# Last scan of a recurrent convolution: columns of the second pair written to the output 32 at a time, in place of store, read back and shuffle

## The chip, the cores and the metric

One core of one Trainium2 chip. The metric is the device time of one execution in microseconds (us), the median of several executions. Times inside the profile are counted from the first instruction of one profiled execution.

## What is computed

The program is four residual layers on x of shape (4, 48, 256, 256), float32: an attention layer, a gated layer, and two layers of directional scans. Only the last of the scan layers matters here. After a group normalisation it runs four scans, each a recurrence with a convolution of width 5 over the 48 channels, and the result is added to x:

```python
def step(w, b):
    def f(carry, inp):
        nxt = inp + _conv1d(carry, w, b)
        return (nxt, nxt)
    return f
...
r0 = ws[0]
_, r_rest = jax.lax.scan(step(right_w, right_b), r0, ws[1:])
R = jnp.concatenate([r0[None], r_rest], 0)
l0 = R[Ww - 1]
_, l_rest = jax.lax.scan(step(left_w, left_b), l0, R[Ww - 2::-1])
L = jnp.concatenate([l0[None], l_rest], 0)[::-1]
return jnp.moveaxis(L, 0, 3)
...
x = x + _L3_conv_ref(_gn(x), ...)
```

The four scans go down the rows, up the rows, right over the columns and left over the columns. Step t needs step t - 1, so one scan of 256 steps is a strict chain. The left scan of the last layer yields the output, column 255 first and column 0 last; the output lies in memory row by row.

## The kernel before

The four images are two pairs of two. A pair has its own `chain` (a Python generator, one `yield` per scan step). A step (`step`, L1037) is done for each of the two images: three matmuls of 96x96 on 96x128 (L1045), a VectorE add of the step's input out of PSUM into one of four carry buffers (L1053 for column scans, L1049 for row scans), and a third operation that keeps the result. The 96 partitions are 48 channels times the parity of the position along the vector; for a column, partition half r holds the rows 2h + r.

The chains are interleaved by hand at the end of `scans` (from L1373). Chain 0 leads by LEAD = 992 steps, then both run alternately, step by step, until chain 0 is done. Chain 1 then runs its last 992 steps alone: nearly all of its last layer, whose left scan comes last.

Instructions go into each engine's queue in an order that a planner works out from the order of the program, from what they depend on and from when buffers come free; it may send a load out earlier than the program has it. All large transfers of this stage are issued by SyncE (SP), on one DMA queue.

The left scan (L1268 to L1306) takes the 256 columns in 16 blocks of 16, block 15 first. Per block it needs two tiles of 96 partitions times 16 KB (1536 KB each): `lines`, the right scan's results, from R (L1273), and `stage`, the layer's input x of the same columns, from x (L1274). Both are asked for a block ahead. In every step GpSimd (POOL) adds the new carry into `stage` in place (L1282), in pieces of 96x128; the elements of one column stand 32 bytes apart in `stage`. When a block is done, `stage` is stored (L1291) to a tensor `y` in memory, in a column-blocked layout with runs of 8 columns (32 bytes) of one row.

`to_rows` (L1337) brings `y` into the row layout of the output. It loads pieces of `y` (`oi`, L1348), shuffles them with copies on POOL, VectorE (DVE) and ScalarE (ACT) into `oo` (L1364 to L1368), and stores `oo` to `out` (L1370). Its arguments choose the pair, the blocks of columns and the buffers. The loop over chain 1 (L1383 to L1397) calls its pieces between steps:

- pair 0, all columns, a piece every 32 steps;
- at step lead - W // 2 = 864, when the left scan of pair 1 is halfway, what is left of pair 0, and from then on the right half of pair 1 (finished by then), a piece every 10 steps;
- after the last step, what is left, and then the left half of pair 1 with the buffers of both pairs.

Buffers: each pair has a ring of five slots of 16 KB a partition (`take`, L1012), and a slot is taken again when its last user is done. While chain 1 runs alone, its own five hold `lines` and `stage`, and those of pair 0 hold `oi` and `oo`. `SLOT` is 4096 elements, `CB` 16 columns, `NK` 16 blocks, `KC` 8.

Of the kernel before, what the change touches and what calls it, by code (L numbers as in the profile page):

```python
# [16 lines left out]
B, C, H, W = 4, 48, 256, 256  # L17
G = 16
NP = 2
# [5 lines left out]
KC = 8  # L25
NK = W // (2 * KC)
# [88 lines left out]
def rows(pair):  # L115
    return slice(pair * P, (pair + 1) * P)
# [848 lines left out]
def scans(ctx, tc, xs, out, wts, biases, dram, k, coefs, lead, spare):  # L965
# [13 lines left out]
    nc = tc.nc  # L979
# [19 lines left out]
    CB = 2 * KC  # L999
    SLOT = 2 * NK * NH * KC  # L1000
# [11 lines left out]
    def take(pair, name):  # L1012
        return buffers[pair].tile([P, SLOT], F32, tag="slot", name=name)

    def chain(pair):
# [8 lines left out]
        def slot(name):  # L1024
            return take(pair, f"{name}{pair}")

        def inner():
            return carry[at[0]][:, :, 1 : HP - 1]
# [27 lines left out]
        def rows_view(t):  # L1056
            return t.rearrange("p (b k h w) -> p b k h w", b=2, k=NK, w=KC)

        def cols_view(t):
            return t.rearrange("p (b q h w) -> p b q h w", b=2, q=2, w=KC)  # L1060

        def lines_view(t):

            return t.rearrange("p (w b h) -> p w b h", w=CB, b=2)

        def row(ts, r):
            return rows_view(ts[r % 2])[:, :, :, r // 2, :]

        def load_rows(layer, n, ts, k0, k1):

            for r in range(2):
                v = rows_view(ts[r])
                for q in range(2):
                    for b in range(2):
                        nc.sync.dma_start(
                            v[q * C : (q + 1) * C, b, k0:k1].rearrange("c k h w -> c k (h w)"),
                            xs[layer][pair][
                                r * C : (r + 1) * C, b, 2 * k0 + q : 2 * k1 - 1 + q : 2, n * NH : (n + 1) * NH, :
                            ].rearrange("c k h w -> c k (h w)"),
                        )  # L1080

        def layer_of(layer, first):
# [6 lines left out]
            block_of = lambda x, n: x[:, :, 2 * n : 2 * n + 2].rearrange("p b q h w -> p b (q h w)")  # L1089
            by_batch = lambda t: t.rearrange("p (b n) -> p b n", b=2)  # L1090
# [3 lines left out]
            for b in range(2):  # L1094
                t = home.tile([P, 2], F32, tag=f"biased{pair}{b}", name="biased", bufs=2)
# [19 lines left out]
            for n in range(NT):  # L1115
                ahead_ = None
                for r in range(RT):
# [3 lines left out]
                    if ahead_ and r >= RT // 2 and r % 4 == 0:  # L1121
                        i = (r - RT // 2) // 4
# [3 lines left out]
                    def keep(new, b):  # L1126
                        nc.scalar.activation(inp[:, b], blocks(new[:, b]), AF.Identity, bias=bias[:, 0:1])  # L1127
# [15 lines left out]
            for n in reversed(range(NT)):  # L1143
                ahead_ = None
                for r in reversed(range(RT)):
# [4 lines left out]
                    if n == 0 and r == RT // 4:  # L1150

                        column = slot("col")
                        v = cols_view(column)
                        for par in range(2):
                            for b in range(2):
                                h0 = NH + 1 - par
# [5 lines left out]
                    i = n * RT + r + 1  # L1162
                    if i == H:
                        continue
                    place = row(now, r)
# [9 lines left out]
                    if n == 0 and r < 2:  # L1175

                        par, h0 = 1 - r, r
                        v = cols_view(column)
# [14 lines left out]
                for r in range(2):  # L1193
                    v = rows_view(now[r])
                    par = 1 - r
                    nh = NH - (r == 1 and n == NT - 1)
                    h0 = n * NH + r
# [19 lines left out]
            x, y = xs[layer][pair], xs[layer + 1][pair]  # L1217
            stage = None
# [11 lines left out]
            for n in range(NK):  # L1230
                ahead_ = None
                for w in range(CB):
# [3 lines left out]
                    if w == 0 and n + 1 == NK:  # L1236
                        stage = slot("stage")
# [27 lines left out]
            if layer == 0:  # L1265
                stats = [wp.tile([P, NK * 4, 6], F32, tag=f"st{pair}{b}", name="st") for b in range(2)]
            following = None
            for n in reversed(range(NK)):  # L1268
                ahead_ = None
                for w in reversed(range(CB)):  # L1270
                    if w == CB - 1 and n > 0:
                        ahead_ = slot("lines"), slot("stage")
                        nc.sync.dma_start(ahead_[0], Rt[n - 1])  # L1273
                        nc.sync.dma_start(by_batch(ahead_[1]), block_of(x, n - 1))  # L1274
                    if layer == 0 and n == 0 and w == CB // 2:
                        following = [slot("dn"), slot("dn")]
                        load_rows(1, 0, following, 1, NK)
                    line = lines_view(lines)[:, w]
                    to = cols_view(stage)[:, :, w % 2, :, w // 2]

                    def keep(new, b):
                        nc.gpsimd.tensor_add(to[:, b], to[:, b], new[:, b])  # L1282

                    if n == NK - 1 and w == CB - 1:
                        keep(inner(), slice(0, 2))
                    else:
                        step(layer, 2, line, keep)
                    if late:
                        late.pop(0)()
                    yield  # L1290
                nc.sync.dma_start(block_of(y, n), by_batch(stage))  # L1291
                if layer == 0:

                    def stat(b, c, n=n, v=by_batch(stage)):
                        nc.vector.bn_stats(stats[b][:, n * 4 + c, :], v[:, b, c * 512 : (c + 1) * 512])

                    late += [lambda b=b, c=c, f=stat: f(b, c) for b in range(2) for c in range(4)]
                    if n == 0:
                        for r in range(2):
                            for q in range(2):  # L1300
                                nc.sync.dma_start(
                                    rows_view(following[r])[q * C : (q + 1) * C, :, 0].rearrange("c b h w -> c b (h w)"),
                                    cols_view(stage)[r * C : (r + 1) * C, :, q, :NH, :].rearrange("c b h w -> c b (h w)"),
                                )
                if ahead_:
                    lines, stage = ahead_  # L1306
# [21 lines left out]
        for layer in range(2):  # L1328
            following = None
            for got in layer_of(layer, first):  # L1330
                if got is None:
                    yield
                else:
                    following = got
            first = following

    def to_rows(pair, k0, nk, of):  # L1337

        y = xs[2][pair]
        nh = SLOT // (nk * CB)  # L1340
        to = out[rows(pair)].rearrange("p (h w) -> p h w", w=W)[:, :, k0 * CB : (k0 + nk) * CB]
        slot = lambda name, i: take(of[i % len(of)], name)
        for n in range(H // 2 // nh):
            got = []
            for r in range(2):
                t = slot("oi", n)
                for b in range(2):
                    nc.sync.dma_start(  # L1348
                        t[b * C : (b + 1) * C].rearrange("c (k n) -> c k n", k=2 * nk),
                        y[  # L1350
                            r * C : (r + 1) * C, b, 2 * k0 : 2 * (k0 + nk), n * nh : (n + 1) * nh, :
                        ].rearrange("c k h w -> c k (h w)"),
                    )
                got.append(t.rearrange("p (k q h w) -> p k q h w", k=nk, q=2, w=KC))
            yield
            for half in range(2):
                o = slot("oo", n)
                v = o.rearrange("p (h r k w q) -> p h r k w q", h=nh // 2, r=2, k=nk, q=2)
                here = slice(half * nh // 2, (half + 1) * nh // 2)
                for i in range(4):  # L1360
                    r, q = i // 2, i % 2
                    dst, src = v[:, :, r, :, :, q], got[r][:, :, q, here, :].rearrange("p k h w -> p h k w")
                    if i == 0 or len(of) == 1 and i < 3:
                        nc.gpsimd.tensor_copy(dst, src)  # L1364
                    elif i == 1 and len(of) > 1:
                        nc.vector.tensor_copy(dst, src)
                    else:
                        nc.scalar.copy(dst, src)  # L1368
                h0 = 2 * n * nh + half * nh
                nc.sync.dma_start(to[:, h0 : h0 + nh, :], o.rearrange("p (h w) -> p h w", w=nk * CB))  # L1370
                yield

    chains = [chain(pair) for pair in range(NP)]  # L1373
# [6 lines left out]
    while next(chains[0], True) is None:  # L1380
        next(chains[1])

    pieces, i = to_rows(0, 0, NK, [0]), 0  # L1383
    for _ in chains[1]:
        i += 1
        if i < lead - W // 2:
            if i % 32 == 0:
                next(pieces, None)
        elif i == lead - W // 2:
            for _ in pieces:  # L1390
                pass
            pieces = to_rows(1, NK // 2, NK // 2, [0])
        elif i % 10 == 0:
            next(pieces, None)
    for rest in (pieces, to_rows(1, 0, NK // 2, [0, 1])):
        for _ in rest:
            pass  # L1397


@with_exitstack  # L1400
# [121 lines left out]
```

## Time and profile before

| what | value |
|---|---|
| median of 3 runs | 9271.56 us (9259.34 to 9274.27) |
| the profiled execution, its time | 9263.67 us |
| its span, first to last instruction | 9261.9 us |
| mean granted TensorE clock | 0.973 |
| busy over the span: PE, DVE, ACT, POOL | 8718.4, 3774.1, 3511.9, 2108.1 us |
| DMA packets, bytes, mean rate | 1058055, 1440.95 MB, 156 GB/s |
| packets under 512 B | 64976 |
| first and last add of the last left scan (L1282) | 8668.0 and 9118.1 us |
| POOL adds L1282, whole program | 2044, mean 521 ns |

How to read it: PE is TensorE's matmul, PEld its weight load, SPq is SyncE as an issuer of DMAs. A group `out<-in` names the tile written and the tiles read. Transfers are named in the same way: `lines<-R` and `stage<-x` are the loads of the left scan, `x<-stage` its store to `y` (which the trace calls x), `oi<-x` and `out<-oo` the load and the store of `to_rows`. "DMA share" is the mean busy share of the core's 16 DMA engines.

### The profile page before, as it was taken

What the parts mean: (1) busy time and instruction counts of PE and PEld (TensorE: products, weight loads), DVE (VectorE), ACT (ScalarE), POOL (GpSimd) and SP (SyncE); (2) the same over time, 40 slices, a digit from 0 to 9 for tenths busy, and PEclk for the clock granted to TensorE, in tenths of its full rate; (3) what the DMA queues carried; (4) which work ended last, traced back from release to release, by engine and by line L of the source; (5) the groups of instructions that cost most, each with busy time, mean ns of one, the idle gap of its engine ahead of it and who ended that gap; (6) DMA issues with size and microseconds to landing.
All of it is one profiled execution on the core that took longest, in us unless ns stands there. A gap on an engine that the chain in (4) does not pass through costs nothing.

```text
span 9261.9 us, 162499 instructions
## 1 busy us (share of the span) xinstructions
PE 8718.4 (94%) x62920; PEld 7269.3 (78%) x62920; DVE 3774.1 (41%) x10798; ACT 3511.9 (38%) x7057; POOL 2108.1 (23%) x3886
## 2 busy tenths in 40 slices
PE   6999999989999888999999999999999999999972
PEld 4777777433333347999999999999999999999972
DVE  3331110335555564444455444444445554434431
ACT  0001000123334456655404766656640027655200
POOL 0000000001111120003572000004457760005662
PEclk9999999999999998999999999999999999999985
DMA  7663322568888868565587845656558879778699
GB/s 149 130 130 86 74 64 68 108 139 171 183 174 181 179 159 173 123 139 142 153 220 156 160 115 134 144 139 160 150 155 219 220 187 184 168 176 216 190 209 198
DMA packets 1058055, 1440.95 MB, mean 156 GB/s; under 512 B 64976, under 2 KB 981200, under 8 KB 991232
## 3 DMA queue, kind: packets, MB, share of 16 engines
q1 hardware_dynamic: 1057184, 1430.23, 67.4%
q8 instruction: 493, 8.08, 0.4%
q14 instruction: 282, 2.31, 0.1%
q0 software_dynamic: 96, 0.33, 0.0%
HBM read 837.19 MB, written 534.77 MB: 148 GB/s over the span
## 4 chain that ended last, share of the span: by engine, by line
PE 86%; DMA 6%; DVE 3%; SPq 2%; POOL 1%; issue 1%; ACT 1%; ACTq 0%; DVEq 0%; POOLq 0%
PE ps L1045 57%; PE py L581 6%; PE acc L294 5%; PE acc L295 5%; PE acc L296 4%; PE py L590 3%; DMA tok<-x 2%; PE pt L276 1%; DMA lines<-R 1%; PE pout L868 1%; PE ph L698 1%; PE ptok L751 1%; DMA oi<-x 1%; DMA sx<-in_x 1%; POOL stage L1282 1%
## 5 line engine op out<-in xcount | busy, mean ns | idle before, releaser
L1045 PE MATMUL ps<-carry,w 96*96 96x128 f32 x48960 | 5495.6, 275 | 143.4 <-DVE carry L1053 109.1
L1045 PEld LDWEIGHTS ps<-carry,w 96*96 96x96 f32 x48960 | 5442.9, 163 | 200.2 <-DVE carry L1053 120.4
L1225 POOL COPY pre<-col 96x256 f32<-96x256 f32 x1020 | 656.7, 645 | 2754.2 <-DMA col<-last 1969.5
L1282 POOL TENSOR_TENSOR stage<-stage,carry 96x128 f32<-96x128 f32 (+1 forms) x2044 | 1053.5, 521 | 479.2 <-DVE carry L1053 217.9
L1248 ACT ACTIVATE lines<-carry,b 96x128 f32<-96x128 f32 (+1 forms) x2044 | 815.7, 401 | 614.9 <-DVE carry L1053 611.1
L1127 ACT ACTIVATE dn<-carry,b 96x128 f32<-96x128 f32 (+1 forms) x2044 | 768.7, 398 | 705.9 <-DVE carry L1049 703.0
L1049 DVE TENSOR_TENSOR carry<-ps,dn 96x128 f32<-96x128 f32 x2280 | 655.2, 288 | 881.4 <-PE ps L1045 794.9
L1053 DVE TENSOR_TENSOR carry<-ps,pre 96x128 f32<-96x128 f32 x2040 | 587.3, 288 | 797.7 <-PE ps L1045 546.7
L1168 ACT ACTIVATE up<-carry,b 96x128 f32<-96x128 f32 x1792 | 718.4, 402 | 481.9 <-DVE carry L1049 480.8
L1053 DVE TENSOR_TENSOR carry<-ps,lines 96x128 f32<-96x128 f32 x2040 | 576.6, 286 | 755.6 <-PE ps L1045 640.9
L1049 DVE TENSOR_TENSOR carry<-ps,up 96x128 f32<-96x128 f32 x1792 | 516.4, 288 | 678.6 <-PE ps L1045 668.4
L581 PE MATMUL py<-x1n,wy 128*96 128x512 f32 x1536 | 700.3, 605 | 30.9 <-ACT x1n L541 28.1
L295 PE MATMUL acc<-xs,xt 128*96 128x288 f32 x2048 | 666.4, 407 | 0.0
L294 PE MATMUL acc<-xt 128*96 128x288 f32 x2048 | 665.8, 408 | 0.0
L581 PEld LDWEIGHTS py<-x1n,wy 128*96 128x96 f32 x1536 | 243.9, 165 | 452.3 <-issue 433.0
L261 ACT ACTIVATE xn<-raw,coef 96x2048 f32<-96x2048 f32 x64 | 133.6, 2094 | 984.6 <-PE pt L276 826.6
L296 PE MATMUL acc<-xt,xs 128*96 128x192 f32 x2048 | 501.7, 327 | 0.0
L279 DVE COPY xt<-pt 128x384 f32<-128x384 f32 x256 | 136.5, 554 | 850.7 <-PE pt L276 651.5
L296 PEld LDWEIGHTS acc<-xt,xs 128*96 128x96 f32 x2048 | 332.1, 164 | 154.2 <-issue 1.2
L295 PEld LDWEIGHTS acc<-xs,xt 128*96 128x96 f32 x2048 | 331.9, 164 | 151.1 <-issue 2.2
L604 DVE TENSOR_TENSOR y<-py,t 96x512 f32<-96x512 f32 x256 | 171.3, 677 | 594.4 <-PE py L590 587.7
L590 PE MATMUL py<-x2n,wy 64*96 64x512 f32 x1536 | 363.0, 601 | 0.0
(179 smaller groups left out, 4656.8 us busy)
## 6 DMA issues: line engine op xcount, KB each, us to landing
stage<-x SPq DMA_DIRECT2D x64, 1536.0 KB
x<-stage SPq DMA_DIRECT2D x64, 1536.0 KB
dn<-x SPq DMA_DIRECT2D x240, 384.0 KB
col<-U SPq DMA_DIRECT2D x60, 1536.0 KB
R<-lines SPq DMA_DIRECT2D x60, 1536.0 KB
lines<-R SPq DMA_DIRECT2D x60, 1536.0 KB
D<-dn SPq DMA_DIRECT2D x56, 1536.0 KB
up<-D SPq DMA_DIRECT2D x56, 1536.0 KB
```

What stands on the lines that cost most here:

```text
L294: nc.tensor.matmul(acc[0], lhsT=xt[:, h + 2, :], rhs=xt[:, here, :], start=first, stop=last)
L295: nc.tensor.matmul(acc[1], lhsT=xt[:, h + 2, :], rhs=xs[:, here, :], start=first, stop=last)
L296: nc.tensor.matmul(acc[2], lhsT=xs[:, h + 2, :], rhs=xt[:, past, :], start=first, stop=last)
L581: nc.tensor.matmul(ps, lhsT=held["w"][0][:, dx], rhs=x1n[:, 2 * c : 2 * c + 2, dx : dx + W], start=dx == 0, stop=False)
L1045: nc.tensor.matmul(ps, lhsT=w_sb[layer][:, way, j, :], rhs=old[:, i, j : j + W // 2], start=j == 0, stop=j == 2)
L1049: nc.vector.tensor_add(new[:, i].rearrange("p (k w) -> p k w", w=KC), ps.rearrange("p (k w) -> p k w", w=KC), inp[:, i])
L1053: nc.vector.tensor_add(new[:, i], ps, inp[:, i])
L1127: nc.scalar.activation(inp[:, b], blocks(new[:, b]), AF.Identity, bias=bias[:, 0:1])
L1168: nc.scalar.activation(place[:, b], blocks(new[:, b]), AF.Identity, bias=bias[:, 1:2])
L1225: nc.gpsimd.tensor_copy(t, cols_view(block)[:, :, w % 2, :, w // 2])
L1248: nc.scalar.activation(line[:, b], new[:, b], AF.Identity, bias=bias[:, 2:3])
L1282: nc.gpsimd.tensor_add(to[:, b], to[:, b], new[:, b])
```

## The change

For the last layer of pair 1 (`direct`), the left scan no longer stores `stage`. For every two blocks it takes two buffers of pair 0's ring, one per image (`done`), each with 32 columns of the image for 128 rows of each parity. POOL's add reads `stage` and the carry as before, and writes its result into `done`, where a row's 32 columns lie together; the elements of one column thus stand 128 bytes apart. When the even block of the two is done, four DMAs (two images, two parities) write them to `out`, in 48 x 128 runs of 32 columns (128 bytes) each. The add of the very first column, one instruction for both images, becomes two.

`to_rows` is used for pair 0 alone; its arguments and its VectorE copy go, and its pieces come every 28 steps. After the last step of chain 1 nothing is left to do but the last four DMAs.

```diff
+            direct = layer == 1 and pair == NP - 1
+            done = None
             for n in reversed(range(NK)):
                 ahead_ = None
+                if direct and n % 2 == 1:
+                    done = [take(0, "done") for _ in range(2)]
                 for w in reversed(range(CB)):
...
                     def keep(new, b):
-                        nc.gpsimd.tensor_add(to[:, b], to[:, b], new[:, b])
+                        if not direct:
+                            nc.gpsimd.tensor_add(to[:, b], to[:, b], new[:, b])
+                            return
+                        for i in range(b.start, b.stop):
+                            place = done[i].rearrange("p (h w) -> p h w", w=2 * CB)[:, :, n % 2 * CB + w]
+                            nc.gpsimd.tensor_add(place, to[:, i], new[:, i])
...
-                nc.sync.dma_start(block_of(y, n), by_batch(stage))
+                if not direct:
+                    nc.sync.dma_start(block_of(y, n), by_batch(stage))
+                elif n % 2 == 0:
+                    for b in range(2):
+                        at_rows = out[(2 * pair + b) * C : (2 * pair + b + 1) * C].rearrange(
+                            "c (h r w) -> c h r w", r=2, w=W
+                        )
+                        for r in range(2):
+                            nc.sync.dma_start(
+                                at_rows[:, :, r, n * CB : (n + 2) * CB],
+                                done[b][r * C : (r + 1) * C].rearrange("c (h w) -> c h w", w=2 * CB),
+                            )
...
-    def to_rows(pair, k0, nk, of):
+    def to_rows(pair):
...
-                    if i == 0 or len(of) == 1 and i < 3:
+                    if i < 3:
                         nc.gpsimd.tensor_copy(dst, src)
-                    elif i == 1 and len(of) > 1:
-                        nc.vector.tensor_copy(dst, src)
                     else:
                         nc.scalar.copy(dst, src)
...
-    pieces, i = to_rows(0, 0, NK, [0]), 0
-    for _ in chains[1]:
-        i += 1
-        if i < lead - W // 2:
-            if i % 32 == 0:
-                next(pieces, None)
-        elif i == lead - W // 2:
-            for _ in pieces:
-                pass
-            pieces = to_rows(1, NK // 2, NK // 2, [0])
-        elif i % 10 == 0:
+    pieces = to_rows(0)
+    for i, _ in enumerate(chains[1]):
+        if i % 28 == 27:
             next(pieces, None)
-    for rest in (pieces, to_rows(1, 0, NK // 2, [0, 1])):
-        for _ in rest:
-            pass
+    assert next(pieces, True) is True
```

More of the change, by code (lines that the diff above doesn't have):

```diff
@@ L1335, in chain @@
             first = following
-    def to_rows(pair, k0, nk, of):
+    def to_rows(pair):
         y = xs[2][pair]
-        nh = SLOT // (nk * CB)
-        to = out[rows(pair)].rearrange("p (h w) -> p h w", w=W)[:, :, k0 * CB : (k0 + nk) * CB]
-        slot = lambda name, i: take(of[i % len(of)], name)
+        nh = SLOT // W
+        to = out[rows(pair)].rearrange("p (h w) -> p h w", w=W)
         for n in range(H // 2 // nh):
@@ L1345, in to_rows @@
             for r in range(2):
-                t = slot("oi", n)
+                t = take(pair, "oi")
                 for b in range(2):
                     nc.sync.dma_start(
[L1349 to L1352, printed above, removed]
+                        t[b * C : (b + 1) * C].rearrange("c (k n) -> c k n", k=2 * NK),
+                        y[r * C : (r + 1) * C, b, :, n * nh : (n + 1) * nh, :].rearrange("c k h w -> c k (h w)"),
                     )
-                got.append(t.rearrange("p (k q h w) -> p k q h w", k=nk, q=2, w=KC))
+                got.append(t.rearrange("p (k q h w) -> p k q h w", k=NK, q=2, w=KC))
             yield
             for half in range(2):
-                o = slot("oo", n)
-                v = o.rearrange("p (h r k w q) -> p h r k w q", h=nh // 2, r=2, k=nk, q=2)
+                o = take(pair, "oo")
+                v = o.rearrange("p (h r k w q) -> p h r k w q", h=nh // 2, r=2, k=NK, q=2)
                 here = slice(half * nh // 2, (half + 1) * nh // 2)
@@ L1369, in to_rows @@
                 h0 = 2 * n * nh + half * nh
-                nc.sync.dma_start(to[:, h0 : h0 + nh, :], o.rearrange("p (h w) -> p h w", w=nk * CB))
+                nc.sync.dma_start(to[:, h0 : h0 + nh, :], o.rearrange("p (h w) -> p h w", w=W))
                 yield
```

## The prediction

> **What bounds the kernel now.** I read first the windows view (busy time of each engine, granted TensorE clock, DMA share, GB/s), cut at three places: the first add of pair 1's last scan (8667), the first long stall (8882), the last add (9118.6).
>
> ```profile
> 8667.00:8882.00 215.00, 215.00 (x1920) 213.82 (x1918) 92.22 (x320) 3.02 (x4) 169.05 (x322) 1.00 0.77 200
> 8882.00:9118.60 236.60, 144.61 (x1148) 142.23 (x1146) 54.87 (x192) 6.45 (x6) 116.17 (x215) 0.79 0.94 214
> 9118.60:9262.00 143.40, 0.00 (x0) 0.00 (x0) 10.57 (x8) 16.24 (x16) 11.46 (x9) 0.50 0.91 187
> ```
>
> The last scan begins bound by PE (busy 215.00 of 215.00), then is bound by the DMA engines (share 0.94), and its last 143.40 us hold no matmul at all. The whole question lies in these 595 us. The waits of PE and of DVE from 8600 on give the stalls, and the chain of waits says what ends them:
>
> ```profile
> PE ps L1045 <- DVE carry L1053: 91.0, 7, 23.6
> DVE carry L1053 <- DMA lines<-R: 86.5, 6, 24.2
> ```
>
> ```profile
> 8910.11 25.24 DMA stage<-x
> ...
> 9035.74 18.69 DMA lines<-R
> 9054.90 16.78 PE ps L1045 x119
> 9071.68 23.27 DMA lines<-R
> 9095.41 22.26 PE ps L1045 x180
> 9118.12 0.53 POOL stage L1282
> 9118.67 7.50 DMA x<-stage
> ...
> 9127.75 19.33 DMA oi<-x
> 9147.32 4.07 ACT oo L1368 x4
> ```
>
> The loads of the scan queue behind the reading back of pair 1's right half; then comes the left half, read, shuffled and written with nothing beside it. The order on the one DMA queue is in SyncE's timeline:
>
> ```profile
> 8688.14 0.55 SPq L1274 DMA_DIRECT2D stage<-x  x1
> 8688.78 0.58 SPq L1291 DMA_DIRECT2D x<-stage  x1
> 8702.38 0.31 SPq L1273 DMA_DIRECT2D lines<-R  x1
> 8709.63 0.55 SPq L1274 DMA_DIRECT2D stage<-x  x1
> ```
>
> Blocks of 16 columns end at 8688.1, 8709.6 and 8731.2: 21.5 us each. The x load for block 13 goes out when block 15 ends, ahead of block 15's store; R loads go out over a block before they are used. Loads are thus issued 1 to 2 blocks early, and a late one is absorbed for about 21 us.
>
> **The price of a packet of 128 B**, which no transfer of this kernel has. Two windows hold nearly one kind of packet only: 32 B runs to HBM (U<-last, 4219 to 4220.9) and 512 B runs to the output (out<-oo, 9247 to 9256).
>
> ```profile
> DMA packets 2645, 0.10 MB, mean 51 GB/s; under 512 B 2616, under 2 KB 2645, under 8 KB 2645
> q1 hardware_dynamic: 2645, 0.10, 72.5%
> ```
>
> ```profile
> DMA packets 4589, 2.34 MB, mean 260 GB/s; under 512 B 16, under 2 KB 4589, under 8 KB 4589
> q1 hardware_dynamic: 4589, 2.34, 101.5%
> ```
>
> 1.9 us x 16 engines / 2645 = 11.5 ns a packet of 32 B; 9 x 16 / 4589 = 31.4 ns one of 512 B.
>
> **The Trainium skill.** "DMA: Bandwidth & Descriptors", Specifications, asks for 512 B or more for line rate and says that below it the engines do a read-modify-write. The trace agrees on the rate (51 against 260 GB/s), but shows no price of a rewrite: the 32 B packet takes about a third of the 512 B one. Same page, Bandwidth (why small descriptors are slow): a fixed overhead of about 3 cycles a packet beside 32 B a cycle, that is 4 + 3 against 16 + 3 cycles for 128 and 512 B, an estimate of 7/19 x 31.4 = 11.6 ns; in the trace the fixed part is larger. "GPSIMD Engine Reference", Performance pitfalls for Q7 kernels: reads of SBUF with a step over 8 bytes cost half as much again; it says nothing of writes. The adds of L1282 already step 32 bytes on both sides (median 521 ns), so the trace neither confirms nor denies it.
>
> **The change, part by part.**
> Removed: (1) the tail, 143.4 us. (2) During the scan, the reading back and shuffling of the right half: 16 oi loads of 768 KB, 8 out stores, POOL copies of about 1 us. PE's idle 91.0 us hang on these; with them goes the restart at a low clock: the scan took 451.6 us, 16 x 21.5 are 344, so 107.6 us are stall and restart. (3) 16 stores x<-stage, some 4 us of queue each. Where the stalls go, what is late next? The new stores.
>
> Added: per two blocks (32 columns) four stores of 48 x 128 = 6144 runs of 128 B, 24,576 packets. A straight line between the two prices gives 11.5 + 19.9 x 96/480 = 15.5 ns; I take 16.3, since half of the stores read the first 48 partitions, from which 512 B stores ran slower in another stage (U<-up: 1677 packets in 8121 to 8126, 47.7 ns each). 24,576 x 16.3 / 16 = 25 us. Bounds: as cheap as 32 B (11.5, 17.7 us), as dear as 512 B (31.4, 48 us). Below 11.5 is excluded, since it carries more bytes than the 32 B packet.
>
> The loads: two per block, 1.57 MB each at the 225 to 229 GB/s that these reads show in this scan (8689 to 8695, 8702.5 to 8709): 6.8 us, 27.2 per two blocks. So two blocks need 25 + 27 = 52 us of queue against 43 us of PE. The queue, not PE, is the bound, from the end of block 14 on.
>
> The end, followed through: after 8709.6 the queue holds 13 loads of x and 12 of R (25 x 6.8 = 170) and seven groups of stores (175) until the group of blocks 3 and 2 has drained: 9054.6. The x load of block 1 lands ahead of that group, of the last x load and of an R load: 9054.6 - 25 - 13.6 = 9016. PE can run some 4 us before it (four carry buffers), so block 1 runs from 9012 to 9033.5 and block 0 to 9055. Then 1 us for POOL, 25 for the last stores, 1.4 from last packet to span end: 9082.5, that is 179 us below 9261.9.
>
> Small edits. POOL's adds now write with a step of 128 B: at 521 ns two of them lie inside PE's 1.345 us a step; if they cost over 670 ns POOL sets the pace. I take nothing; the bounds are 0 and 48 us (850 ns, case E below). SyncE now issues 32 stores in place of 16 and stands blocked while their runs drain; it also waits some 1 us for POOL's last add of every second block. Behind it stand only loads of the same queue, counted above. The buffers of pair 0 rotate over five, so a group must land within about two blocks of its issue: at 52 us a cycle the wait is about zero. The adds of the very first column become two: 0.2 us. Pair 0's pieces, every 28 steps in place of 32, press 902 us of transfers (7658 to 8560) into some 790, beside a PE that idled only 21.8 us from 7560 to 8667 (its longest stall 10.8). Their loads and stores move past U<-up, col<-U and R<-lines on SyncE's queue, their copies past `pre` on POOL and the bias adds on ACT, which were busy 232 and 649 of 1070 us from 7597 to 8667: taken as zero, bounds -10 and +10.
>
> Sum: 9263.7 (the profiled execution's own time) - 179 = 9084.4. The runs' median, 9271.56, lies 8 us above that execution, so I forecast 9092.
>
> **The rivals.**
> A, likeliest (0.55): the queue bounds the scan at 48 to 58 us per two blocks, as above: 9092, own range 9070 to 9150.
> B (0.15): packets near 11.5 ns. Two blocks need 45 us, hidden but for crumbs; PE sets the pace: 8667 + 344 + 2 for the stall crumbs + 1 + 17.7 + 2 = 9034, with the same 2 and 8 us added 9044. For it: 32 B runs at 11.5 with the engines only 72.5% busy.
> C (0.12): the order on SyncE turns round and both loads of the next block go out behind the stores. R lands 32 us after the end of a block, x 38.6, PE restarts at 34.6, 13 us late, plus 2 for the clock: 7 x 15 = 106 us of stalls; 8667 + 344 + 106 + 28 = 9145, as a median 9155. Against it: the order shown above.
> D, the other side (0.10): writes of 128 B into HBM cost more than the whole 512 B packet. The point of decision is 31.4 ns: 170 + 8 x 48 us after 8709.6 ends at 9264, no gain. At 45 ns a group takes 69 us, and the end is 8709.6 + 170 + 8 x 69 + 1.4 = 9433, as a median about 9443: slower. For it: the skill's rewrite below 512 B, and that 6144 runs at a step of 2 KB are another address pattern than any here. Against it: 2616 runs of 32 B, just as partial, at 11.5 ns.
> E (0.05): POOL's strided writes at 850 ns: 8667 + 435 + 28 = 9130, as a median 9140.
> 0.03 is left for an end within 0.2% from sizes of A and D meeting.
>
> **Numbers.** About 0.2% (19 us) is what a measurement can tell from no change. Faster: A, B, C, E, 0.87; within: 0.04, with D's near edge; slower: 0.09. Range: down to B's end (9040); up to 9200, where a group takes 39 us (25.5 ns a packet). It leaves out most of D.
>
> **What would show it.** A: some 196,600 more packets under 512 B; about 1000 of them a microsecond while stores drain; DMA share near 1 from 8710 on; short waits of DVE on lines<-R or of POOL on stage<-x every second block; a tail of about 27 us after the last add. B: PE without gaps. C: loads issued after the stores in SyncE's timeline. D: packets of 128 B over 31 ns. E: DVE waiting on POOL in every step. It is wrong if the stretch before 8667 moves by more than 10 us, or if a packet's price lies outside 11.5 to 31.4 ns.

## The result and the profile after

The changed kernel takes 9152.29 us, the median of 4 runs (9142.75 to 9156.64), beside 9271.42 for the kernel before: a ratio of 0.9875, 95% interval 0.9862 to 0.9887. It is 119 us faster, where 179 had been forecast (9092), and it lies inside the range of 9040 to 9200. The profiled execution took 9152.88 us, with a span of 9151.1.

The windows view of the changed kernel (busy time of PE, PEld, DVE, ACT and POOL, granted clock, DMA share, GB/s), cut at the start of the last scan, at the end of its second block, at its last add and at the end:

```profile
8687.60:8729.90 42.30, 42.30 (x379) 42.16 (x378) 18.16 (x63) 0.79 (x2) 32.76 (x63) 1.00 0.50 116
8729.90:9121.70 391.80, 319.55 (x2685) 317.19 (x2683) 129.15 (x448) 0.00 (x0) 229.14 (x449) 0.90 0.83 158
9121.70:9151.10 29.40, 0.00 (x0) 0.00 (x0) 0.00 (x0) 0.00 (x0) 0.48 (x1) 0.56 0.74 107
```

The tail without matmuls has shrunk from 143.4 us to 29.4. But from the end of the second block on PE again stands still, and now at a DMA share of only 0.83: something waits although the DMA engines are not full. (The share adds up the times of the packets, and can pass 1 where these overlap.) The waits from 8600 on name it:

```profile
POOL done L1293 <- DMA stage<-x: 105.6, 7, 15.9
DVE carry L1053 <- POOL done L1293: 84.6, 22, 11.7
...
PE ps L1045 <- DVE carry L1053: 71.7, 7, 11.1
```

Read upwards: PE waits for DVE, DVE for a carry buffer that POOL has not read, POOL for the x load, seven times. R loads (`lines<-R`) are waited for no more. After such a wait PE also starts again at a lower granted clock (the last number but two), as two windows after the first wait show:

```profile
8769.00:8771.00 2.00, 2.00 (x11) 2.00 (x11) 0.58 (x2) 0.00 (x0) 2.00 (x5) 0.50 0.79 180
8775.00:8779.00 4.00, 4.00 (x38) 3.98 (x37) 1.69 (x7) 0.00 (x0) 3.12 (x6) 1.00 1.13 254
```

It is 0.50 for some 6 us after the wait, and then 1.00 again as before it. The scan's 434 us are 90 more than the 344 of an unhindered PE: 71.7 of waits, and about 18 left over for the seven restarts. SyncE's timeline shows where the x load stands:

```profile
8708.43 0.55 SPq L1280 DMA_DIRECT2D stage<-x  x1
8709.08 0.54 SPq L1279 DMA_DIRECT2D lines<-R  x1
8729.85 20.66 SPq L1310 DMA_DIRECT2D out<-done  x4
8750.61 5.51 SPq L1280 DMA_DIRECT2D stage<-x  x1
8756.16 0.59 SPq L1279 DMA_DIRECT2D lines<-R  x1
```

At the end of block 15 x and R loads go out at once. At the end of block 14 the four stores go out first, and SyncE is held by issuing them: the x load of block 12 follows 20.7 us later. Block 12 could have begun at 8750.8; the chain of waits has its x load land at 8766.3:

```profile
8750.61 15.71 DMA stage<-x
...
8766.45 0.53 POOL done L1293
...
8767.34 40.46 PE ps L1045 x332
```

To compare executions, the table cuts each profiled one at three events in the trace: the hand-over (the last matmul of line L96, with which chain 0 ends), the first and the last add of the last scan. What lies ahead of the hand-over is the same work in all of them and scatters between 7545 and 7566 us.

| us | hand-over to first add | last scan | after the last add |
|---|---|---|---|
| before | 1119.1 | 450.2 | 143.8 |
| changed | 1134.5 | 434.0 | 29.4 |

The tail gave 114 us and the scan 16; the stretch ahead of the scan took 15 back (and the hand-over itself lay 4 us later in this execution).

### The profile page after: what moved, and what is told of

It is laid out like the page before. It is cut to its first block, busy times and chain, and to the rows that moved or that the text cites. A ratio compares the mean times of both kernels' runs of the same rounds, so it can differ in the third digit from the quotient of the medians.

```text
span 9151.1 us, 162340 instructions
## 1 busy us (share of the span) xinstructions
PE 8728.1 (95%) x62920; PEld 7283.8 (80%) x62920; DVE 3763.0 (41%) x10790; ACT 3489.5 (38%) x7033; POOL 2073.9 (23%) x3855
## 4 chain that ended last, share of the span: by engine, by line
PE 89%; DMA 4%; DVE 3%; ACT 2%; issue 1%; SPq 1%; POOL 1%; DVEq 0%; POOLq 0%; ACTq 0%
PE ps L1045 58%; PE py L581 7%; PE acc L294 5%; PE acc L295 5%; PE acc L296 4%; PE py L590 4%; PE pt L276 1%; DMA stage<-x 1%; DMA tok<-x 1%; PE ph L698 1%; ACT x1n L541 1%; PE pout L868 1%; PE ptok L751 1%; DMA x<-y 1%; DMA sx<-in_x 1%
## 5 line engine op out<-in xcount | busy, mean ns | idle before, releaser
L1049 DVE TENSOR_TENSOR carry<-ps,dn 96x128 f32<-96x128 f32 x2280 | 655.2, 288 | 892.9 <-PE ps L1045 803.3
L1289 POOL TENSOR_TENSOR stage<-stage,carry 96x128 f32<-96x128 f32 (+1 forms) x1533 | 793.1, 521 | 312.3 <-DVE carry L1053 184.2
L1049 DVE TENSOR_TENSOR carry<-ps,up 96x128 f32<-96x128 f32 x1792 | 516.4, 288 | 678.3 <-PE ps L1045 668.9
```

The lines of the kernel that those rows point to most:

```text
L1049: nc.vector.tensor_add(new[:, i].rearrange("p (k w) -> p k w", w=KC), ps.rearrange("p (k w) -> p k w", w=KC), inp[:, i])
```

## The experiments

The theories that they were to tell apart. O: the order on SyncE's queue makes PE wait. T: two blocks need so much DMA time that the order is of no account. P: the denser pieces of pair 0 cost the 15 us ahead of the scan. Each ratio is to the kernel before, timed beside the run on the same chip.

**pace30.** Pair 0's pieces every 30 steps.

```diff
-        if i % 28 == 27:
+        if i % 30 == 29:
```

> The changed kernel with pair 0's pieces every 30 steps in place of 28. Its last scan begins at 8687.6 us, that of the kernel before at 8668.0. Theory P (the denser pieces cost the 20 us: their transfers crowd the row loads of the down scan): about half of it comes back, the last scan begins near 8678 and the median falls by 5 to 12 us, to about 9143. Rival Q (the 20 us come from something else, such as the planner's other order): the start stays within 3 us of 8687 and the time at 9152.

Measured: 9146.83 us, ratio 0.9869 (0.9855 to 0.9882). Inconclusive: the median fell by 5.5 us, but the intervals overlap with the changed kernel's, and the profiled execution, which at 9161.72 was some 15 us above the others, had 1143 us from the hand-over to the scan.

**before28.** The kernel before, with this one number of the change alone.

```diff
-            if i % 32 == 0:
+            if i % 28 == 0:
```

> The kernel before with pair 0's pieces every 28 steps in place of 32, nothing else. Theory P: its last scan begins near 8688 in place of 8668, and the time rises by 15 to 20 us to about 9289. Rival Q: it stays at 9271 within 5 us.

Measured: 9286.44, ratio 1.0016 (1.0009 to 1.0024), and 1134.3 us from the hand-over to the first add, as in the changed kernel. P holds. (The last scan began at 8700.6 rather than 8688, since the hand-over lay 17 us later in this execution.) The waits of PE in that stretch show where, first of the kernel before, then of before28:

```profile
PE ps L1045 <- DVE carry L1053: 11.2, 2, 10.8
PE ps L1045 <- DVE carry L1049: 6.4, 6, 1.8
PE ps L1045 <- DVE carry L1252: 4.2, 1, 4.2
```

```profile
PE ps L1045 <- DVE carry L1049: 12.0, 10, 2.1
PE ps L1045 <- DVE carry L1252: 11.5, 1, 11.5
PE ps L1045 <- DVE carry L1053: 10.6, 2, 9.7
```

L1049 is the row scans, L1252 the start of the right scan, which waits for its first block of columns: there the wait grows from 4.2 to 11.5 us, and that of the row scans from 6.4 to 12.0. Together PE waits 12.3 us longer, most of the 15.

**act_queue.** The stores issued by ACT, whose DMA queue is another one.

```diff
-                            nc.sync.dma_start(
+                            nc.scalar.dma_start(
```

> The changed kernel with the stores out<-done issued by ACT, whose queue is another one, so that the loads of the scan no longer stand behind them on SyncE's. Theory O (order: PE waits because the x load of the next block stands behind a group of stores): the seven waits of about 10 us fall to 0 to 3 us, and the time falls by 50 to 70 us to 9085 to 9100. Theory T (throughput: two blocks need some 27 us of stores and 27 us of loads, 54 of the 56 us of a cycle): the waits only move, the cycle stays at 53 to 56 us and the time falls by 0 to 25 us, to 9127 to 9152.

Measured: 9087.23, ratio 0.9801 (0.9788 to 0.9815); the scan takes 380.2 us in place of 434.0. O holds, and T as I put it falls. But the scan is not at PE's own 344 us either. The windows of 112 us from 8730 and 8842, and the waits in its last scan:

```profile
8730.00:8842.00 112.00, 112.00 (x1001) 111.78 (x1000) 47.98 (x167) 0.00 (x0) 85.76 (x167) 1.00 1.06 200
8842.00:8954.00 112.00, 97.05 (x842) 96.59 (x841) 40.32 (x141) 0.00 (x0) 71.59 (x140) 0.92 1.03 192
```

```profile
POOL done L1293 <- DMA out<-done: 31.8, 2, 19.8
...
PE ps L1045 <- DVE carry L1053: 30.7, 3, 15.0
```

No wait for an x load is left. The DMA engines are full (1.06 and 1.03), the loads come in time, the stores fall behind, and twice POOL waits for a `done` buffer that is not written out yet. So T names the bound that comes next.

**long_runs.** The same buffers stored as they lie, in runs of 16 KB.

```diff
-                                at_rows[:, :, r, n * CB : (n + 2) * CB],
-                                done[b][r * C : (r + 1) * C].rearrange("c (h w) -> c h w", w=2 * CB),
+                                out[(2 * pair + b) * C : (2 * pair + b + 1) * C, (n + r) * SLOT : (n + r + 1) * SLOT],
+                                done[b][r * C : (r + 1) * C],
```

> The changed kernel with the same buffers stored as runs of 16 KB, in the order they have in the buffer: it leaves out the row order of pair 1's output, so its time shows what the 128 B runs cost beside the same bytes. Both theories: a group of stores takes about 8 to 13 us in place of 27, the waits of PE in the last scan go, a pair of blocks takes 43 to 45 us, the tail falls from 29 to about 11 us. Time 9152 - 72 of waits - 18 of restarts - 18 of tail, about 9045. If 16-engine time is not what the small runs cost (theory O with its price in the queue's order alone), a wait of some 3 to 5 us per group stays and the time is 9070 to 9090.

Measured: 9050.11, ratio 0.9764 (0.9750 to 0.9777); scan 344.1 us, tail 16.2. One line of PE's timeline holds the whole scan:

```profile
8357.47 674.68 PE L1045 MATMUL ps<-carry,w 96*96 96x128 f32 x5928 [9.95 <-DVE carry L1053]
```

There is no gap from 8357 to 9032, with the stores still ahead of the x loads. This kernel leaves out the row order of pair 1's output; beside it the small runs cost 102 us of the changed kernel: 90 in the scan, where loads stand behind them, and 13 in the tail, which at 16.2 us is 5 longer than expected.

**late_stores.** The stores put four steps into the next block in the program, still on SyncE's queue.

```diff
-                            nc.sync.dma_start(
-                                at_rows[:, :, r, n * CB : (n + 2) * CB],
...
+                            held.append(
+                                lambda b=b, r=r, n=n, done=done, at_rows=at_rows: nc.sync.dma_start(
...
+                    if w == CB - 4:
+                        while held:
+                            held.pop(0)()
```

> The changed kernel with each group of stores put four steps into the next block in the program (the last group at once), still on SyncE's queue. Theory O (order): the loads of the next blocks get ahead of the stores, PE's seven waits of 10 us shrink to 0 to 4 us, and as the DMA engines were 0.88 busy in a cycle of 56 us, the cycle falls to 49 to 51 us: 9152 - 35 to 49 = 9103 to 9117. Rival S (ACT's queue helped because small and large packets of two queues fill each other's gaps, DMA share 1.03 to 1.07, and not because of the order): one queue keeps its share of 0.88 to 0.92 and the time falls by 0 to 20 us, to 9132 to 9152.

Measured: 9106.53, ratio 0.9826 (0.9813 to 0.9840); scan 384.1 us. The planner left the stores at the block's end; what changed is that the x load goes out ahead of them, as SyncE's timeline shows for the second group:

```profile
8772.17 0.56 SPq L1281 DMA_DIRECT2D stage<-x  x1
8772.83 34.45 SPq L1315 DMA_DIRECT2D out<-done  x4
8807.33 5.47 SPq L1280 DMA_DIRECT2D lines<-R  x1
```

So it is in all the groups that follow; of the first, one store in four still goes out before the x load. The R load stands behind. That alone takes PE's waits in the scan from 71.7 us to 26.6, now for x and R by turns, and the DMA share from 0.88 (56 us windows of the changed kernel) to 0.98:

```profile
8730.00:8842.00 112.00, 105.84 (x914) 105.15 (x913) 43.68 (x152) 0.00 (x0) 77.08 (x153) 0.95 0.98 187
```

```profile
PE ps L1045 <- DVE carry L1053: 26.6, 10, 5.9
```

Rival S (two queues fill each other's gaps) is not needed for most of the gain. O holds. Whether the x load of the changed kernel lost its time while SyncE was held by issuing the stores, or behind them on the queue, these runs do not separate.

**half_runs.** A group of stores after each block, in runs of 64 B.

```diff
-                elif n % 2 == 0:
+                else:
...
-                                at_rows[:, :, r, n * CB : (n + 2) * CB],
-                                done[b][r * C : (r + 1) * C].rearrange("c (h w) -> c h w", w=2 * CB),
+                                at_rows[:, :, r, n * CB : (n + 1) * CB],
+                                done[b][r * C : (r + 1) * C].rearrange("c (h w) -> c h w", w=2 * CB)[
+                                    :, :, n % 2 * CB : (n % 2 + 1) * CB
+                                ],
```

> The changed kernel with a group of stores after every block, 16 columns each: the same bytes in twice the packets, of 64 B. If a packet has a fixed price (11.5 ns at 32 B, 15.8 and 14.0 ns at 128 B in the two kinds of stores): about 13.5 ns each, 49,152 packets x 13.5 / 16 = 41 us for two blocks in place of 27, so a cycle of 56 + 14 = 70 us and 9152 + 7 x 14 - 8 (a last group of 20 us in place of 28) = about 9240. If the price is one of bytes in the end, the cycle stays at 56 and the time within 10 us of 9145.

Measured: 9205.02, ratio 0.9933 (0.9919 to 0.9947); scan 497.3 us, some 66 us for two blocks. That lies between the two expectations and nearer to a fixed price per packet: 63 us more of scan for the same bytes. But the price is not fixed. The last group of stores stands alone on the queue, with the same number of packets as in the changed kernel; the stretches after the last add, first of the changed kernel (29.4 us), then of half_runs (21.5 us):

```profile
DMA packets 24640, 3.15 MB, mean 107 GB/s; under 512 B 24640, under 2 KB 24640, under 8 KB 24640
```

```profile
DMA packets 24681, 1.58 MB, mean 73 GB/s; under 512 B 24681, under 2 KB 24681, under 8 KB 24681
```

Half the bytes in as many packets take about three quarters of the time. An estimate for a full queue: of the 66.4 us that two blocks take on average (12 groups of stores, from 8749.7 to 9114.9) 27.2 are loads by the prediction's sum, and the rest is 12.8 ns for each of 49,152 packets. A straight line between the prediction's prices for 32 and 512 B gives 12.8 too; with the 13.5 ns that had been assumed, two blocks came to 70.

**split_queues.** Parity 0 stored from SyncE, parity 1 from ACT.

```diff
-                            nc.sync.dma_start(
+                            (nc.sync, nc.scalar)[r].dma_start(
```

> The changed kernel with the stores of parity 0 (partitions 0 to 47, some 1015 packets a us and a thin end) on SyncE's queue and those of parity 1 (partitions 48 to 95, 1140 a us) on ACT's, side by side. Theory O: half the stores still stand ahead of the x load, so half of the wait stays, 3 to 6 us a cycle, and the time falls by 25 to 45 us, to 9107 to 9127. If it is the thin end of the parity 0 stores that costs (2 x 2.5 us a group), two kinds side by side fill it and the time comes near ACT's 9087.

Measured: 9126.16, ratio 0.9849 (0.9836 to 0.9863); scan 410.0, PE's waits 48.4 us. Half of the stores ahead of the x load leave part of the wait, as O says, though more than it said: 6.9 us a time rather than 3 to 6, and the gain is at the lower edge of what was expected.

**sp_pace and act_pace.** The changed kernel and act_queue with another pace of pair 0's pieces.

```diff
-        if i % 28 == 27:
+        if i % 32 == 31 if i < 512 else i < 736 and (i - 512) % 24 == 23:
```

> The changed kernel with pair 0's pieces every 32 steps in the first 512 steps and every 24 in the next 224, nothing else. Theory P: the stretch from the hand-over of the chains to the first add of the last scan falls from 1134 us to near the 1119 of the kernel before, and the time from 9152 to 9132 to 9140. Rival: the pace is of no account and the 15 us come from the planner's other order; the time stays within 6 us of 9152.

> The changed kernel with the stores on ACT's queue (9087 us) and pair 0's pieces every 32 steps in the first 512 steps and every 24 in the next 224. Theory P (pieces at 28 steps crowd the down scan): the last scan begins 14 to 20 us earlier, 9067 to 9075. Rival: the denser pieces in the right scan stall its loads as much, and the time stays within 6 us of 9087.

Measured: sp_pace 9134.67, ratio 0.9850 (0.9836 to 0.9863), 1117.4 us from the hand-over to the first add: P again. act_pace 9082.41, ratio 0.9803 (0.9790 to 0.9817): the stretch fell to 1117.5, yet the time missed 9067 to 9075 and its ratio was no better than act_queue's, measured on another chip. So both were run on one:

> The kernel of act_queue once more, beside act_pace on one chip, since the two were timed in different calls: 9081 to 9092.

> The kernel of act_pace beside act_queue_b. Its profile had its last scan begin 17 us sooner after the hand-over of the chains, as theory P says; if that counts, it is 12 to 20 us faster than act_queue_b. If the two lie within 6 us, the wait for the stores takes the gain back.

Measured: act_queue_b 9090.09, ratio 0.9815 (0.9801 to 0.9828); act_pace_b 9079.02, ratio 0.9798 (0.9784 to 0.9811). By the medians the pace is worth 11 us here, between the two expectations, and the intervals of the ratios overlap; the scan is 380.6 us in both. By its median act_pace_b is the fastest version that leaves nothing out, 73 us under the changed kernel, but the ratios do not set it apart from act_queue.

**late_pace.** late_stores with that pace.

> The kernel of late_stores (x load ahead of the stores) with that pace as well: the two things in which the changed kernel differs from what was assumed before it ran. If they add up: 9106 - 15 to 20 = 9086 to 9091, which is where the forecast of 9092 lay. If they don't: above 9098.

Measured: 9096.28, ratio 0.9808 (0.9794 to 0.9821), with 1120.4, 388.5 and 29.8 us for the three stretches. By the median it lies 5 us above what was expected if the two add up, and 2 under what was expected if they don't. The kernel before was slower beside it, too (9273.54 in place of 9266.36), and by the ratio the pace gained 17 us over late_stores, with intervals that overlap. In the profiles the pace gives 14 us ahead of the scan, and the scan takes 4 back. So the two add up for the most part.

## Why the prediction was right, and where it was not

The direction was right, and so was the main part of the mechanism: the tail and the stalls of the right half went, and what came next was the new stores. The step that failed is the order on the queue, and one small term, the pace of pair 0's pieces, was taken as zero.

**The price of a packet.** Right. 24,640 packets under 512 B pass after the last add, and one group takes about 27 us where I had 25. The two halves differ as supposed: in the changed kernel, stores of parity 0 (from the first 48 partitions; 8732 to 8735) and of parity 1 (8739.5 to 8743):

```profile
DMA packets 3036, 0.39 MB, mean 130 GB/s; under 512 B 3036, under 2 KB 3036, under 8 KB 3036
```

```profile
DMA packets 3961, 0.52 MB, mean 147 GB/s; under 512 B 3960, under 2 KB 3960, under 8 KB 3960
```

That is 15.8 and 14.1 ns. What the 16.3 did not hold is the thin end of the parity 0 stores: when few packets are left, the DMA engines are only half busy (a share of 53.8% from 8735.5 to 8738.5). Over 8730 to 8757 the average comes to 27 x 16 / 24,650 = 17.5 ns. With a full queue a group costs less: in late_stores, from the third group of stores to the seventh, two blocks take 51.2 us, where the sum had 52; with 27.2 of loads that leaves 24, or 15.6 ns a packet, as an estimate. Why the thin ends cost less there was not tried. Rival D falls: the read-modify-write of which the Trainium skill speaks below 512 B ("DMA: Bandwidth & Descriptors", Specifications) shows no price here beyond that of a short packet, about half a 512 B packet's 31.4 ns. Whether the engines do it at all, no run shows.

**The loads.** In the window of an x and an R load after block 15 (8709 to 8720) they ran at 222 GB/s, near the 225 to 229 of the sum, and late_stores' cycle of 51.2 us bears the sum out.

**The order on the queue.** This step failed. "The x load for block 13 goes out when block 15 ends, ahead of block 15's store" was read from the kernel before and carried over to the new stores. In the changed kernel the stores of every second block went out ahead of the x load. So the bound from block 14 on was not a full queue, as case A, the likeliest, has it, but an x load that came late to a queue with time to spare: the DMA share is 0.83, where A's sign was a share near 1. It is rival C in a milder form: x alone is late, not R, and PE waits 10.2 us seven times rather than 13. late_stores puts the x load back in front and has a scan of 384.1 us; the sum of the prediction gave 388 (from 8668 to 9056). The misplaced order cost 434.0 - 384.1 = 50 us. Why the planner chose it stays open; in the kernel before, the x load had led the store by only 0.6 us.

That two blocks took about 56 us, inside A's 48 to 58, is luck: that room, and the range up to 9200, had been made for dearer packets and not for waits. C's number, 9155, comes nearest to the measured one, in part by chance: its 106 us of stalls and restarts were 90, and what was missing came from the stretch ahead of the scan, which C did not have.

**The pieces of pair 0.** "Taken as zero, bounds -10 and +10" was too narrow: before28 and sp_pace both put it at 15 to 18 us. By the prediction's own sign (the stretch before 8667 moves by more than 10 us) it is wrong here. The working looked at how long PE had idled in the stretch (21.8 us in 1107), not at how near the waits were to growing when the same transfers are packed closer.

**POOL's adds.** Right: median 520 ns with a step of 128 B, 521 before. The Trainium skill, "GPSIMD Engine Reference", Performance pitfalls for Q7 kernels, speaks of reads only; between writes with a step of 32 B and of 128 B the traces show no difference, and in no run does this add write with a step of 8 B or less. Rival E falls.

**The sum.** A span of 9082.5 us was worked out, and the profiled one is 9151.1, or 68.6 more. The scan took 46 us more than the sum's 388, the stretch ahead of it 15 more, the tail 3 more, and the hand-over lay 4 us later. With order and pace put back, late_pace has a scan of 388.5 us and a ratio of 0.9808; 9092 / 9271 is 0.9807. That they agree so closely is chance, as the executions of late_pace alone differ by 10 us. Rival B, with PE alone setting the pace, needs cheaper runs: long_runs shows it.

## What to carry to other kernels

Ask of a transfer that is dear in packets, not in bytes, which load stands behind it on its queue. Moving one 1.5 MB load in every two blocks in front of the stores was worth 46 us here, a second queue 65. The second queue does not make the stores free: in act_queue PE still waited 30.7 us in the scan, nearly all of it for buffers that were not written out yet. An order seen in a trace belongs to that program; when an edit changes when buffers come free, the order of the new program has to be looked at, or be enforced, before a time is built upon it. And background work that is moved closer together can have a price even beside an engine that is 98% busy.

## What was not expected of the hardware

In this kernel the time of a short packet follows a straight line rather well: 11.5 ns at 32 B and 31.4 at 512 B measured, 12.8 at 64 B and 15.6 at 128 B as estimated above for a full queue. A packet of 32 B thus costs over a third of one with sixteen times the bytes.

With stores on one queue and loads on the other, the loads can win by far: in act_queue, while two loads run (8732 to 8740), the stores' queue (q10) moves 167 packets in 8 us, beside some 1000 a microsecond when it is alone.

```profile
q1 hardware_dynamic: 170, 1.88, 103.0%
q10 hardware_dynamic: 167, 0.02, 3.2%
```

In this window the two queues move nearly as many packets as each other, but one of the loads' holds 11 KB on average (1.88 MB / 170) and one of the stores' 128 B. In other windows the counts differ (177 and 56 from 8772 to 8778), so turns of one packet each are not shown.
